# A two-layer graph transformer on one core: a longer weight ring from layer 1's output projection on, with tiles shared to make room, and PSUM banks and index work of layer 1's end in another order

## The chip, the core and the metric

The kernel runs on one core of a Trainium2 chip. The metric is device time in microseconds for one execution; below, "before" is the median of three executions. A core has five engines with instruction queues of their own: TensorE (PE in the profile, its weight loads PEld), VectorE (DVE), ScalarE (ACT), GpSimd (POOL) and SyncE (SP). Each queue is worked off in order; an instruction that waits holds up all behind it. DMA transfers are issued from the queues of SP, ACT and POOL and run beside the engines.

## The reference, cut to what matters

Everything is float32. There are 384 nodes with 1024 features and 12,288 edges. Each of two layers has a graph part, an attention-like part and a mixture of 8 experts. The change lies in the end of layer 0's experts and in layer 1:

```python
# layer 1 (x: 384 x 1024)
h     = normed(x) @ W                                   # graph attention, weights from edge counts
x    += elu(attention(h, a, src, dst))
q, k  = sigmoid(xn @ W_Q), sigmoid(xn @ W_K);  v = xn @ W_V
m     = linear_attention(q, k, v) @ W_fc + xn           # xn: the normed x from the layer's start
x    += gamma * normed(m) + beta
f     = normed(x);  e = argmax(f @ centroids.T)         # one expert of 8 for each node
g     = sigmoid(max(f @ centroids.T))
xe    = normed(f) * gamma[e] + beta[e]
out   = x + f + g * (relu(xe @ w1[e] + b1[e]) @ w2[e] + b2[e])
```

An expert's w1 is 1024 x 512 and its w2 is 512 x 1024: 2 MiB each, 16 such weights in layer 1's experts.

## The kernel before, in words

Nodes lie in three blocks of 128 (`nb`), features in 8 chunks of 128 (`kc`) or two halves of 512 (`hf`).

**Weights.** All large weights pass through a ring of SBUF places of 16 KB a partition (2 MiB in all). `next_w` (L103) takes the place at the front of the ring and moves it to the back; `load_w` (L117) and `load_t` (L107) issue one transfer into it from SyncE. A transfer may start when the last matmul that read the place's former weight is done. Three places are there from the start; `w_top` adds one, `w_more` two, so layer 1 runs with six. When the loads of the output projection `w_fc` have been written (L1145), the pool `mid` is closed (L1146), which frees the tiles that layer 1's middle needed, and a seventh place, `w_last`, is opened in their space (L1148, `LAST = 1`) and put at the front of the ring. The experts open an eighth, `w_end` (L1333), at the back; it lies where layer 1's tiles were and must wait until they are free.

Which instruction stands where in an engine's queue is decided by the Tile framework's scheduler when the program is built, from its estimate of when each can run; so SyncE's loads are not in the order of the source. `tc.issue_after(i)` asks it to put what follows behind instruction `i`. Tiles with the same tag in a pool share buffers, and a tile in a pool that opens over a closed one waits for the users of the closed pool.

**The end of layer 0's experts** (`experts0_sorted`, L889). Expert outputs go to DRAM (`yg0`), ordered by expert; each node gathers its two rows back with indirect DMAs from POOL (`take`, L984: two gathers and two VectorE multiply-adds, L989). For the second half of the features, the last two experts' outputs stay on chip and are added by matmuls with one-hot matrices `back` (L1032); the other experts' rows are gathered at the start of layer 1, block by block (L1039), and then normed (L1043, L1044), transposed and copied to `xnT` (L217), and multiplied by `W` (L1049).

**Layer 1's end.** For each block: two halves of the output projection (`project`, L1151), then `to_router` (L1182: norm, transposes to `xT`, scores against the centroids, moments, the twice-normed row `xn1` and the once-normed row `ft`), then `to_places` (L1205: best expert, place in the sorted order, scatter of the row to DRAM table `xg`; POOL then adds `ft` to `x`, L1224; for the last block VectorE does it, L1252). `to_first` (L1226) sorts the first 128 rows on chip by matmuls into two PSUM banks `first`; `scaled` (L997) multiplies by gamma and adds beta, the first half on VectorE (L1003, L1004), the second on ScalarE (L1010), into `xe0`. The values and node numbers of all sorted rows are scattered to DRAM table `ig`.

**Layer 1's experts** (`experts1_sorted`, L1331) run in four pairs. A pair's 128 rows (64 places for each of two experts) are loaded from `xg` by POOL (L1346), transposed (L1355) and scaled; pair 0's come from `xe0`. `hidden_of` (L1359) computes h with 16 matmuls (L1364; the profile shows two records for each), `hs` is its copy (half on VectorE, L1367, half on ScalarE, L1368), `by_feature` transposes it (L1376) and applies bias and relu, `give` (L1387) multiplies by w2 (y, L1395) and scatter-adds each half to `out` (L1398, L292). Around pair 0: `inf` is loaded from `ig`, three gathers fetch each node's b2 (L307), VectorE computes the target rows `half` (L1410) and adds b2 to `x` (L1412), and ScalarE stores x to `out` (L1414), block by block, ahead of the scatter-adds.

The PSUM pools of the experts are opened in the order transposes (4 banks), h (2), y (2), over layer 1's `pm` (4 banks, projections) and `px` (4 banks; `first` is among them).

Of the kernel before, what the change touches and what calls it, by code (L numbers as in the profile page):

```python
# [10 lines left out]
F32 = mybir.dt.float32  # L11
# [26 lines left out]
LAST = 1  # L38
# [7 lines left out]
def gps_two_layers(ctx: ExitStack, tc: tile.TileContext, d, out: bass.AP):  # L46
# [140 lines left out]
    def norm_on_act(dst, src, mean, rinv):  # L187

        off = small.tile([P, 1], F32, tag="off", name="off")
        ve.tensor_scalar(off, mean, rinv, -1.0, op0=OP.mult, op1=OP.mult)  # L190
        ac.activation(dst, src, AF.Identity, bias=off, scale=rinv)
# [62 lines left out]
    def gate_to_t(pool, tag, gate):  # L254
        gT = small.tile([X, N], F32, tag="gT", name="gT", bufs=1)
        ps = pool.tile([P, HB], F32, tag=tag, name="mm")
        for nb in range(NB):
            nc.tensor.transpose(ps[:X, nb * P:(nb + 1) * P], gate[:, nb, :], ident)
        ve.tensor_copy(gT, ps[:X, :N])
        return gT  # L260
# [153 lines left out]
    with ExitStack() as layer:  # L414
# [317 lines left out]
        def row(cols, name, dtype=F32):  # L732
# [4 lines left out]
                "slots": row([NB, 2], "slots6", I32), "share": row([2, NB], "share6"), "back": row([BACK, N], "back6"),  # L737
# [105 lines left out]
    def experts0_all():  # L843
        with tc.tile_pool(name="act1", bufs=1) as act, \
# [20 lines left out]
            gT = gate_to_t(pb, "b", oh[0])  # L865
# [23 lines left out]
    def experts0_sorted(keep):  # L889

        slots, share = keep["slots"], keep["share"]
        with tc.tile_pool(name="act6", bufs=1) as act, \
                tc.tile_pool(name="work6", bufs=2) as work, \
                tc.tile_pool(name="ps_t6", bufs=3, space=PSUM) as pt, \
                tc.tile_pool(name="ps_h6", bufs=5, space=PSUM) as ph:
# [35 lines left out]
            def ways_back():  # L931
# [19 lines left out]
                for e in range(BACK):  # L951
                    ac.copy(keep["back"][:, e, :], ps[e][:, :N])

            xeT = rows_of(0)
# [8 lines left out]
            for hf in range(2):  # L963
# [15 lines left out]
                if hf == 0:  # L979
                    for nb in range(NB):  # L980
                        yt = work.tile([P, 2, HB], F32, tag="yt", name="yt6", bufs=3)
                        take(hf, nb, yt, slots, share, X * CAP0)

# [13 lines left out]
    def scaled(dst, src, g, es):  # L997

        if g == 0:
            gm, bt = [gbx[:, i, es[0]:es[0] + 2, :4].rearrange("p r k -> p k r")[:, :, :, None].to_broadcast([P, 4, 2, CAP])  # L1000
                      for i in range(2)]
            to, of = [t.rearrange("p k (r c) -> p k r c", r=2) for t in (dst, src)]
            ve.tensor_tensor(to, of, gm, OP.mult)  # L1003
            ve.tensor_tensor(to, to, bt, OP.add)  # L1004
            return
        for j in range(4):
            for r, e in enumerate(es):
                cs = slice(r * CAP, (r + 1) * CAP)
                gm, bt = gbx[:, 0, e, 4 + j:5 + j], gbx[:, 1, e, 4 + j:5 + j]
                ac.activation(dst[:, j, cs], src[:, j, cs], AF.Identity, bias=bt, scale=gm)  # L1010

    def layer1(keep=None):


        with tc.tile_pool(name="act2", bufs=1) as act, \
# [5 lines left out]
            a_bc = act.tile([P, 2, D], F32, tag="rows", name="a_bc")  # L1021
            ed_w = part.tile([P, NB, N], F32, name="ed_w")
# [3 lines left out]
            hn = act.tile([P, NB, KC * K2V], F32, tag="rows3", name="hn")  # L1026
            ws = [load_w(d["w_gnn"][hf]) for hf in range(2)]
            taken, backs = None, []
            for nb in range(NB if keep is not None else 0):
                backs.append(px.tile([P, HB], F32, tag="x", name="back"))  # L1030
                for e in range(BACK):
                    mm(backs[nb], lhsT=keep["back"][:, e, nb * P:(nb + 1) * P],  # L1032
                       rhs=keep["xe0"][e].rearrange("p a b -> p (a b)"), start=e == 0, stop=e == BACK - 1)
            for nb in range(NB):
                with ExitStack() as behind:
                    if nb:
                        behind.enter_context(tc.issue_after(normed_half.ins))
                    if keep is not None:
                        taken = take(1, nb, work.tile([P, 2, HB], F32, tag="xn", name="yt1"),  # L1039
                                     keep["slots_g"], keep["share_g"], (X - BACK) * CAP0)  # L1040
# [30 lines left out]
            gb = act.tile([P, 2, D], F32, tag="rows", name="gb")  # L1071
            for i, n in enumerate(("gamma", "beta")):
                ac.dma_start(gb[:, i, :], bass.AP(tensor=d[n].tensor, offset=d[n].offset, ap=[[0, P], [1, D]]))

            kn = act.tile([P, NB, D], F32, tag="kq", name="kn")
# [14 lines left out]
            for b in range(NB):  # L1090
# [13 lines left out]
                gp.tensor_tensor(x[:, b, :], x[:, b, :], gb[:, 1, :], OP.add)  # L1104


            vn = act.tile([P, NB, KC * K2V], F32, tag="rows3", name="vn")
# [6 lines left out]
            kv = part.tile([P, KC, K2V], F32, name="kv")  # L1114
# [11 lines left out]
            qT = act.tile([P, KC, N], F32, tag="kq", name="qT2")  # L1126
# [32 lines left out]
            def mix_norm(nb):  # L1159
# [3 lines left out]
                for hf in range(2):  # L1163
                    cs = slice(hf * HB, (hf + 1) * HB)
                    ve.scalar_tensor_tensor(y[:, cs], xb[:, cs], mean, gb[:, 0, cs], op0=OP.subtract, op1=OP.mult)  # L1165
# [9 lines left out]
            ft = act.tile([P, NB, KC * K2V], F32, tag="rows3", name="ft4")  # L1175
            xT = act.tile([P, KC, N], F32, tag="kq", name="xT4")
# [5 lines left out]
            def to_router(nb):  # L1182
                mix_norm(nb)
                xs, xb, fb = x[:, nb, :], xn1[:, nb, :], ft[:, nb, :D]
                to_t(pm, xT, xs, nb)
                ps = px.tile([P, HB], F32, tag="x", name="x")
                for kc in range(KC):
                    mm(ps[:, :X], lhsT=xT[:, kc, nb * P:(nb + 1) * P], rhs=cen[:, kc, :],
# [13 lines left out]
                norm_on_act(fb, xs, mean, rinv)  # L1202
                sums[nb] = (ps, less, rinv)

            def to_places(nb):  # L1205
                xb, fb = xn1[:, nb, :], ft[:, nb, :D]
# [15 lines left out]
                if nb < NB - 1:  # L1222
                    with tc.issue_after(last[0].ins):
                        gp.tensor_tensor(x[:, nb, :], x[:, nb, :], fb, OP.add)  # L1224
# [27 lines left out]
            ve.tensor_tensor(x[:, NB - 1, :], x[:, NB - 1, :], ft[:, NB - 1, :D], OP.add)  # L1252
# [5 lines left out]
    def experts1_all():  # L1258
        with tc.tile_pool(name="act3", bufs=1) as act, \
# [41 lines left out]
            gT = gate_to_t(pb, "b", gate)  # L1301
# [29 lines left out]
    def experts1_sorted(xe0):  # L1331

        with tc.tile_pool(name="w_end", bufs=1) as w_end, \  # L1333
                tc.tile_pool(name="act4", bufs=1) as act, \
                tc.tile_pool(name="work5", bufs=2) as work, \
                tc.tile_pool(name="ps_t4", bufs=4, space=PSUM) as pt, \
                tc.tile_pool(name="ps_h4", bufs=2, space=PSUM) as ph, \
                tc.tile_pool(name="ps_y4", bufs=2, space=PSUM) as py:
            ring.append(w_end)
            inf = act.tile([P, X // 2, 2], F32, name="inf4")  # L1340
            half = act.tile([P, 2, X // 2], I32, name="half4")
            b2 = act.tile([P, NB, D], F32, name="b24")

            def load_rows(pair):
                xs = work.tile([P, D], F32, tag="xs", name="xs4", bufs=3)
                gp.dma_start(xs, xg[pair * P:(pair + 1) * P, :])  # L1346
                return xs

            def rows_of(pair):
                xeT = [work.tile([P, KC // 2, P], F32, tag=f"xeT{g}", name="xeT4") for g in range(2)]  # L1350
                for g in range(2):
# [4 lines left out]
                    scaled(xeT[g], ps, g, (2 * pair, 2 * pair + 1))  # L1356
                return xeT

            def hidden_of(pair, xeT):  # L1359
# [6 lines left out]
                hs = work.tile([P, F1], F32, tag="hs", name="hs4")  # L1366
# [4 lines left out]
            def by_feature(pair, hs):  # L1371
                hT = work.tile([P, F1 // P, P], F32, tag="hT", name="hT4")
# [14 lines left out]
            def give(pair, hT, between=None):  # L1387

                w2 = [load_w(d["xw2s"][e], (F1 // P, D)) for e in (2 * pair, 2 * pair + 1)]
                for hf in range(2):  # L1390
# [9 lines left out]
                    if hf == 0 and between is not None:  # L1400
                        got = rows_of(between)
                return got if between is not None else None

            xss = [None] + [load_rows(pair) for pair in range(1, X // 2)]
            gp.dma_start(inf, ig.rearrange("(a p) b -> p a b", p=P))
            for nb in range(NB):
                gather(b2[:, nb, :], d["b2"], keep["own_e"][:, nb:nb + 1], X)
            hs = hidden_of(0, xe0)
            for hf in range(2):
                ve.tensor_scalar(half[:, hf, :], inf[:, :, 1].bitcast(I32), 2.0, float(hf), op0=OP.mult, op1=OP.add)  # L1410
            for nb in range(NB):
                ve.scalar_tensor_tensor(x[:, nb, :], b2[:, nb, :], keep["info"][:, nb, 0:1], x[:, nb, :],  # L1412
                                        op0=OP.mult, op1=OP.add)
                ac.dma_start(out[nb * P:(nb + 1) * P, :], x[:, nb, :])  # L1414
            xeT = give(0, by_feature(0, hs), 1)
# [116 lines left out]
```

## Time and profile before

| | us |
|---|---|
| runs: median, lowest, highest | 1063.69, 1062.56, 1065.06 |
| the profiled execution: its time | 1065.01 |
| its span, first to last instruction | 1063.2 |
| TensorE busy in the span | 1023.2 |
| layer 1, from the first `back` matmul to pair 0's h | 700.9 to 979.1 |
| layer 1's experts, from pair 0's h to the last y | 979.1 to 1054.3 |
| from the last y to the span's end | 8.9 |

How to read what follows: a line of the timeline has the start and the length of a group of instructions in us from the span's start, the engine, the line in the source, the operation, what is written `<-` what is read, the shape and the number of instructions. In brackets stands how long the engine was idle before, and what ended that. A line of the waits has the waiting engine and line, what it waited for, the sum in us, how often and the longest. A line of the windows has the stretch, its length, the busy time of PE, PEld, DVE, ACT and POOL with the number of instructions, then the granted TensorE clock (1.00 is full), the busy share of the 16 DMA engines and the GB/s that they moved.

### The profile page before, as it was taken

The page shows a single profiled execution, that of the slowest core. Times are in us where ns is not written, and L with a number is a line of the kernel's source. Part 1 is how long each engine was busy: PE and PEld are TensorE (multiplying, and loading weights), DVE is VectorE, ACT ScalarE, POOL GpSimd, SP SyncE. Part 2 cuts the span into 40 slices and gives each one's busy share as a digit, 9 for nine tenths or more (in the row PEclk, how much of TensorE's full clock was granted, in tenths as well). Part 3 has the DMA queues.
Part 4 walks back from the last instruction along what each step waited for, and adds up shares of the span by engine and source line. Part 5 has one row for each costly group of instructions (what it writes and reads, how often), then busy time and mean ns, then how long its engine had stood idle before and what let it go on. Part 6 is the DMA issues. An engine that isn't in the chain of part 4 may idle for free. (4 is left out here: it accounts for less than half of the span.)

```text
span 1063.2 us, 9534 instructions
## 1 busy us (share of the span) xinstructions
PE 1023.2 (96%) x3455; PEld 557.6 (52%) x3455; DVE 356.4 (34%) x991; ACT 271.0 (25%) x501; POOL 325.2 (31%) x277
## 2 busy tenths in 40 slices
PE   6999999999999999999998999989999999998895
PEld 5555555554555555544466666434444465555352
DVE  4580000006666666711343111061306000474321
ACT  3111111110876666611121011221302010123120
POOL 2142466556686768510001000140002000013121
PEclk9999999999999999999997999989999999998999
DMA  9939523334425232533265898978522222425994
GB/s 345 393 141 365 154 80 100 139 105 99 80 1 118 42 80 1 159 86 123 92 210 201 305 311 293 380 265 291 198 80 79 80 80 79 158 74 198 398 383 118
DMA packets 69526, 182.84 MB, mean 172 GB/s; under 512 B 21488, under 2 KB 22352, under 8 KB 69216
## 3 DMA queue, kind: packets, MB, share of 16 engines
q1 hardware_dynamic: 40640, 146.01, 38.4%
q0 software_dynamic: 25120, 28.88, 11.6%
q10 hardware_dynamic: 3712, 7.27, 1.8%
q8 instruction: 29, 0.48, 0.2%
q14 instruction: 25, 0.20, 0.1%
HBM read 160.22 MB, written 22.44 MB: 172 GB/s over the span
## 5 line engine op out<-in xcount | busy, mean ns | idle before, releaser
L480 POOL DMA_INDIRECT countd<-seen,cells x96 | 154.3, 1608 | 64.3 <-DMA countd<-seen,cells 38.5
L135 PE MATMUL mm<-xnT,w 128*128 128x384 f32 x512 | 165.7, 486 | 0.1
L135 PEld LDWEIGHTS mm<-xnT,w 128*128 128x128 f32 x512 | 97.1, 190 | 67.6 <-DVE xnT L217 0.3
L666 PE MATMUL mm<-xnT,w 128*128 128x384 f32 x384 | 132.4, 493 | 0.0
L480 POOL DMA_INDIRECT lastd<-typ,cells x96 | 96.6, 1006 | 107.6 <-DMA lastd<-typ,cells 68.7
L666 PEld LDWEIGHTS mm<-xnT,w 128*128 128x128 f32 x384 | 70.5, 190 | 56.4 <-issue 13.4
L714 PE MATMUL mm<-w,t 128*128 128x512 f32 x192 | 84.3, 595 | 0.8 <-DVE x L402 0.8
L147 PE MATMUL mm<-w,xnT 128*128 128x512 f32 x192 | 82.8, 592 | 0.0
L135 PE MATMUL mm<-t,w 128*128 128x384 f32 x256 | 82.7, 486 | 0.0
L917 PE MATMUL h<-w,xeT 128*128 128x352 f32 x224 | 68.5, 462 | 0.6 <-DVE xeT L909 0.3
L135 PEld LDWEIGHTS mm<-t,w 128*128 128x128 f32 x256 | 48.6, 190 | 33.9
L147 PEld LDWEIGHTS mm<-w,xnT 128*128 128x128 f32 x192 | 36.3, 190 | 45.5 <-issue 45.5
L714 PEld LDWEIGHTS mm<-w,t 128*128 128x128 f32 x192 | 35.9, 190 | 44.1 <-issue 42.2
L586 DVE TENSOR_TENSOR kind<-last 128x1152 f32<-128x1152 f32 x1 | 1.4, 1358 | 165.7 <-DMA last<-lastd 165.7
L917 PEld LDWEIGHTS h<-w,xeT 128*128 128x128 f32 x224 | 41.8, 190 | 23.7 <-DVE xeT L909 2.1
L292 POOL DMA_INDIRECT xg<-xn,slot x3 | 4.0, 1342 | 140.4 <-DVE xn L1165 135.4
L1049 PE MATMUL mm<-w,xnT 128*128 128x512 f32 x96 | 44.9, 629 | 1.5 <-DVE xnT L217 1.5
L1154 PE MATMUL mm<-w,oT 128*128 128x512 f32 x96 | 42.6, 595 | 0.0
L969 PE MATMUL y<-w,hT 128*128 128x512 f32 (+1 forms) x96 | 41.6, 593 | 0.0
L147 PE MATMUL mm<-w,t 128*128 128x512 f32 x96 | 41.4, 592 | 0.0
L527 ACT ACTIVATE t<-mm,cols 128x384 f32<-128x384 f32 x24 | 14.0, 582 | 107.1 <-PE mm L135 102.5
L1104 POOL TENSOR_TENSOR x<-x,gb 128x1024 f32<-128x1024 f32 x3 | 7.3, 2427 | 100.8 <-DVE x L1103 100.8
(315 smaller groups left out, 1221.7 us busy)
## 6 DMA issues: line engine op xcount, KB each, us to landing
w<-in_w1s SPq DMA_DIRECT2D x16, 1408.0 KB
w<-in_xw SPq DMA_DIRECT2D x8, 2048.0 KB
w<-in_xw2s SPq DMA_DIRECT2D x8, 2048.0 KB
w<-in_w2s SPq DMA_DIRECT2D x8, 1536.0 KB
keys<-keyd POOLq DMA_DIRECT2D x4, 1536.0 KB
xg<-blank SPq DMA_DIRECT2D x12, 512.0 KB
xs<-xg POOLq DMA_DIRECT2D x10, 512.0 KB
w<-in_wk SPq DMA_DIRECT2D x2, 2048.0 KB
```

The source lines that it names most:

```text
L135: mm(ps[:, :N], lhsT=w[:, j, kc, :], rhs=rhs[:, kc, :], start=kc == 0, stop=kc == KC - 1)
L147: mm(ps, lhsT=lhs[:, kc, nb * P:(nb + 1) * P], rhs=w[:, kc, :], start=i == 0 and kc == 0, stop=i == len(pairs) - 1 and kc == KC - 1)
L292: i = gp.indirect_dma_start(rows, bass.IndirectOffsetOnAxis(ap=at, axis=0), src, None, bounds_check=n - 1, oob_is_err=False, compute_op=op)
L480: gp.indirect_dma_start(cells[:, :], bass.IndirectOffsetOnAxis(ap=at[:, i, c:c + 1], axis=0), src[:, c:c + 1], None, bounds_check=N * N + ...
L527: ac.activation(dst[:, ob, :], ps, AF.Identity, bias=cols[:, i, ob:ob + 1], scale=1.0)
L666: mm(ps[:, :N], lhsT=w[:, j, kc, :], rhs=xnT[:, kc, :], start=kc == 0, stop=kc == KC - 1)
L714: mm(pss[hf], lhsT=src[:, kc, nb * P:(nb + 1) * P], rhs=w_out[("mwo", "wo")[part]][hf][:, kc, :], start=part == 0 and kc == 0, stop=part = ...
L917: mm(ag[i][:, :F0], lhsT=xeT[kc // 4][:, kc % 4, :], rhs=w1[kc // 4][:, kc % 4, i * F0:(i + 1) * F0], start=kc == 0, stop=kc == KC - 1)
L969: mm(y, lhsT=hT[:k, e, j, :], rhs=w2[:k, e % 2 * len(K2) + j, :], start=j == 0, stop=j == len(K2) - 1)
L1049: mm(ps, lhsT=xnT[:, kc, nb * P:(nb + 1) * P], rhs=ws[hf][:, kc, :], start=kc == 0, stop=kc == KC - 1)
L1104: gp.tensor_tensor(x[:, b, :], x[:, b, :], gb[:, 1, :], OP.add)
L1154: mm(ps, lhsT=oT[:, kc, nb * P:(nb + 1) * P], rhs=ws[hf][:, kc, :], start=kc == 0, stop=kc == KC - 1)
```

## The change

- `LAST` becomes 3, and `w_end` goes. From layer 1's output projection on the ring has nine places, all but three of them as before; the three `w_last` stand at the front.
- To make room, tiles move into `mid` and share: `a_bc` with `kn` and `qT`; `hn` and `vn`; `ed_w` with `kv`. `gamma` and `beta` are two tiles, loaded by POOL behind the last gather instead of by ScalarE. `back` shares the tile `own` and one more. `xT` is a work tile of one block. `ft` goes: `add_normed` computes x + f in place on ScalarE, as x * (rinv + 1) - mean * rinv, so the adds on POOL (L1224) and VectorE (L1252) go.
- In layer 0's experts and in layer 1's, the PSUM pools are opened in another order: h's and y's banks first, the transposes' last.
- Block 0's gather of the second half (`take_back`) moves from layer 1 to the end of layer 0's experts.
- In layer 1's experts, pair 1's rows are transposed right after pair 0's `by_feature` and before pair 0's w2 matmuls; `half`, the b2 adds and the stores of x come behind the scaling of pair 1's first half, and the stores move to SyncE. The rows of pairs and the b2 gathers share four buffers, so the rows of pairs 2 and 3 are loaded after pair 1's are used. `hs` and `hT` have one buffer instead of two.

```diff
-LAST = 1
+LAST = 3
...
-    def norm_on_act(dst, src, mean, rinv):
+    def add_normed(x, mean, rinv):
         off = small.tile([P, 1], F32, tag="off", name="off")
         ve.tensor_scalar(off, mean, rinv, -1.0, op0=OP.mult, op1=OP.mult)
-        ac.activation(dst, src, AF.Identity, bias=off, scale=rinv)
+        more = small.tile([P, 1], F32, tag="more", name="more")
+        ve.tensor_scalar(more, rinv, 1.0, None, op0=OP.add)
+        ac.activation(x, x, AF.Identity, bias=off, scale=more)
...
-                tc.tile_pool(name="ps_t6", bufs=3, space=PSUM) as pt, \
-                tc.tile_pool(name="ps_h6", bufs=5, space=PSUM) as ph:
+                tc.tile_pool(name="ps_h6", bufs=5, space=PSUM) as ph, \
+                tc.tile_pool(name="ps_t6", bufs=3, space=PSUM) as pt:
...
+            take_back(work.tile([P, D], F32, tag="xs", name="yt1").rearrange("p (a b) -> p a b", b=HB), 0)
+
+    def take_back(yt, nb):
+        return take(1, nb, yt, keep["slots_g"], keep["share_g"], (X - BACK) * CAP0)
...
-            a_bc = act.tile([P, 2, D], F32, tag="rows", name="a_bc")
-            ed_w = part.tile([P, NB, N], F32, name="ed_w")
+            ed_w = part.tile([P, NB, N], F32, tag="ed", name="ed_w")
...
-            hn = act.tile([P, NB, KC * K2V], F32, tag="rows3", name="hn")
+            hn = part.tile([P, NB, KC * K2V], F32, tag="rows3", name="hn")
+            a_bc = part.tile([P, NB, D], F32, tag="kq", name="a_bc")[:, :2, :]
...
-                        taken = take(1, nb, work.tile([P, 2, HB], F32, tag="xn", name="yt1"),
-                                     keep["slots_g"], keep["share_g"], (X - BACK) * CAP0)
+                        if nb:
+                            taken = take_back(work.tile([P, 2, HB], F32, tag="xn", name="yt1"), nb)
...
+            gamma, beta = act.tile([P, D], F32, name="gamma"), part.tile([P, D], F32, name="beta")
+            with tc.issue_after(taken.ins) if taken else ExitStack():
+                for to, n in ((gamma, "gamma"), (beta, "beta")):
+                    gp.dma_start(to, bass.AP(tensor=d[n].tensor, offset=d[n].offset, ap=[[0, P], [1, D]]))
...
-                norm_on_act(fb, xs, mean, rinv)
+                add_normed(xs, mean, rinv)
...
-                if nb < NB - 1:
-                    with tc.issue_after(last[0].ins):
-                        gp.tensor_tensor(x[:, nb, :], x[:, nb, :], fb, OP.add)
...
-            ve.tensor_tensor(x[:, NB - 1, :], x[:, NB - 1, :], ft[:, NB - 1, :D], OP.add)
...
-        with tc.tile_pool(name="w_end", bufs=1) as w_end, \
-                tc.tile_pool(name="act4", bufs=1) as act, \
+        with tc.tile_pool(name="act4", bufs=1) as act, \
                 tc.tile_pool(name="work5", bufs=2) as work, \
-                tc.tile_pool(name="ps_t4", bufs=4, space=PSUM) as pt, \
                 tc.tile_pool(name="ps_h4", bufs=2, space=PSUM) as ph, \
-                tc.tile_pool(name="ps_y4", bufs=2, space=PSUM) as py:
-            ring.append(w_end)
+                tc.tile_pool(name="ps_y4", bufs=2, space=PSUM) as py, \
+                tc.tile_pool(name="ps_t4", bufs=4, space=PSUM) as pt:
...
-            xss = [None] + [load_rows(pair) for pair in range(1, X // 2)]
+            xss = {1: load_rows(1)}
             gp.dma_start(inf, ig.rearrange("(a p) b -> p a b", p=P))
             for nb in range(NB):
-                gather(b2[:, nb, :], d["b2"], keep["own_e"][:, nb:nb + 1], X)
+                b2s.append(work.tile([P, D], F32, tag="row", name="b24", bufs=4))
+                gather(b2s[nb], d["b2"], keep["own_e"][:, nb:nb + 1], X)
+            xss.update({pair: load_rows(pair) for pair in (2, 3)})
             hs = hidden_of(0, xe0)
-            for hf in range(2):
-                ve.tensor_scalar(half[:, hf, :], inf[:, :, 1].bitcast(I32), 2.0, float(hf), op0=OP.mult, op1=OP.add)
-            for nb in range(NB):
-                ve.scalar_tensor_tensor(x[:, nb, :], b2[:, nb, :], keep["info"][:, nb, 0:1], x[:, nb, :],
-                                        op0=OP.mult, op1=OP.add)
-                ac.dma_start(out[nb * P:(nb + 1) * P, :], x[:, nb, :])
-            xeT = give(0, by_feature(0, hs), 1)
+            hT = by_feature(0, hs)
+            xeT = rows_of(1)
+            with tc.issue_after(scaled_by[0].ins):
+                for hf in range(2):
+                    ve.tensor_scalar(half[:, hf, :], inf[:, :, 1].bitcast(I32), 2.0, float(hf), op0=OP.mult, op1=OP.add)
+                for nb in range(NB):
+                    ve.scalar_tensor_tensor(x[:, nb, :], b2s[nb], keep["info"][:, nb, 0:1], x[:, nb, :],
+                                            op0=OP.mult, op1=OP.add)
+                    nc.sync.dma_start(out[nb * P:(nb + 1) * P, :], x[:, nb, :])
+            give(0, hT)
```

## The prediction

> **What bounds the kernel now.** I read the page first, then TensorE's waits, then the timelines of the stretches where it waits, last the windows with the DMA share.
>
> ```profile
> span 1063.2 us, 9534 instructions
> PE 1023.2 (96%) x3455; PEld 557.6 (52%) x3455; DVE 356.4 (34%) x991; ACT 271.0 (25%) x501; POOL 325.2 (31%) x277
> ```
>
> TensorE is busy for 96% and the change takes no matmul away. All that it can win is among the 40.0 us of idle time and in stretches at half clock. TensorE's waits after 800 us:
>
> ```profile
> PE t L1376 <- issue: 3.9, 1, 3.9
> PE h L1364 <- ACT xe L1010: 2.6, 1, 2.6
> PE first L1228 <- DVE slot L1219: 1.7, 2, 1.2
> PE y L1395 <- SPq L1430: 1.7, 1, 1.7
> ```
>
> Three of these lie in the last experts, which the change rebuilds. TensorE's timeline there (start, length, [idle before]):
>
> ```profile
> 979.08 8.78 PE L1364 MATMUL h<-w,xe 128*64 128x512 f32 x32 [2.57 <-ACT xe L1010]
> 991.72 0.84 PE L1376 MATMUL t<-ident,hs 128*128 128x128 f32 x4 [3.86 <-issue]
> ...
> 1002.26 7.03 PE L1364 MATMUL h<-w,xeT 128*64 128x512 f32 x32
> ...
> 1042.81 0.84 PE L1376 MATMUL t<-ident,hs 128*128 128x128 f32 x4 [0.94 <-DVE hs L1367]
> 1043.69 1.93 PE L1395 MATMUL y<-w,hT 128*64 128x512 f32 x4
> 1047.28 7.05 PE L1395 MATMUL y<-w,hT 128*64 128x512 f32 x28 [1.65 <-SPq L1430]
> ```
>
> Pair 0's h takes 8.78 us where pair 1's takes 7.03. "issue" before 991.72 is explained by VectorE's timeline: the copy of hs stands in its queue behind half, which needs inf from DRAM.
>
> ```profile
> 975.65 1.22 DVE L1252 TENSOR_TENSOR x<-x,ft 128x1024 f32<-128x1024 f32 x1
> 976.79 0.68 DVE L1004 TENSOR_TENSOR xe<-xe,gbx 128x512 f32<-128x512 f32 x1
> 991.05 0.24 DVE L1410 TENSOR_SCALAR half<-inf 128x4 int32<-128x4 int32 x2 [13.58 <-DMA b<-in_b,own_e]
> 991.20 0.42 DVE L1367 COPY hs<-h 128x256 f32<-128x256 f32 x1
> ```
>
> The last wait (1.65 us) is for pair 3's second w2. The windows (last two columns: DMA share, GB/s) show why it is late:
>
> ```profile
> 905.00:950.00 45.00, 44.21 (x175) 25.32 (x175) 25.70 (x88) 7.35 (x12) 1.92 (x2) 1.00 0.27 94
> 950.00:978.00 28.00, 24.44 (x132) 18.70 (x130) 17.81 (x69) 9.58 (x18) 9.30 (x6) 0.88 0.55 207
> 978.00:988.00 10.00, 8.78 (x32) 2.61 (x32) 0.00 (x0) 1.03 (x4) 4.50 (x7) 0.83 0.97 313
> 988.00:1046.50 58.50, 52.87 (x236) 24.53 (x236) 17.12 (x37) 12.64 (x44) 11.57 (x8) 0.97 1.00 372
> ```
>
> From 978 to 1046.5 the DMA engines have no free time; from 905 to 978 they have much. So the tail has two limits close together: TensorE's chain, and the bytes that may only be asked for when a place comes free.
>
> **The change, part by part.** *Places.* Before, SyncE issues w2 of pair 1 at 977.26 (the place w_end opens only when layer 1's pools close) and pair 2's first w1 at 987.89. So 9 tiles of 2.1 MB cross the full stretch. In the built order of the changed program, SyncE issues pair 0's w1, w1 and w2 into the three shared places at about 912 (the release of before's w_last: 912.34), and the places that they would have taken go to later tiles. Pair 1's last w2 goes at 951.6, pair 2's first w1 at 961.4, when out-projection weights are done. From the end of pair 0's h on, 7 tiles are left instead of 9. The two go where the share was 0.27 to 0.55.
>
> *Pair 0's h.* Its PSUM bank comes from a pool that no longer overlaps first, and L1252 is gone from VectorE. Pair 0's first half is ready at 975.05 + 0.69 + 0.68 = 976.4, plus 0.12 for the new small operation more (three of them, like L1196's 0.15 us rows; two are hidden under projection matmuls); TensorE ends first at 976.5 + 0.1. The second half on ScalarE ends at 979.0 as before, when 16 of the 32 matmul records have 3.5 us of work. So h starts at 976.6: 2.5 us won. The in-place activation of x costs what L191 does now (1.23 us, same shape). Two adds on POOL (2.38 us each) go and were hidden.
>
> *Clock.* The page "TensorE: Matmul & The Clock Gate" of the Trainium skill (HAM oscillation) asks for no idle gap over about 3.4 us; a gap of 2.57 us would then cost its own length alone. The trace says otherwise: 713 ns a record in pair 0's h against 592 in the others, clock 0.83 in that window, so 8.78 against 7.03. I take the row, 1.75 us won; by the rule it is 0, and the total below shrinks by 1.7. The end of h moves from 987.86 to 983.6.
>
> *half.* It is placed behind pair 1's scaling, so hs is copied at once: the wait 3.86 becomes pair 3's 0.94; 2.9 us won. Then hs transposes 0.84, xs transposes 1.76 (now ahead of y), y 7.3 as in pair 1, against 10.54 us from 991.72 to 1002.26: about 0.7 us won, again clock. Pair 1's h starts at 994.4 instead of 1002.26. Pair 1's rows are issued at 979 as now, and land near 983 on idle DMA engines; they are needed at 985.3.
>
> *TensorE's chain after that* is unchanged: 41.4 us from pair 1's h to pair 3's y. So y could start at 1035.8 instead of 1043.69.
>
> *Supply.* Bytes from 978 to 1046.5: 10 x 313 + 58.5 x 372 = 24.9 MB, of which 9 tiles are 18.9 and rows, gathers, stores and scatters 6.0. From 983.6 on, 7 tiles (14.7) and about 5.4 of the others are left: 20.1 MB at 372 GB/s is 54.0 us, to 1037.6. Now 0.7 us lie between the last packets and 1047.28; so TensorE resumes at 1038.3 instead of 1047.28: 9.0 us won, with a stall of some 2.5 us left. The page "DMA: Bandwidth & Descriptors" (Specifications) gives about 358 GB/s of HBM to a core; that would mean 56.1 us, and 2.1 less won. The row is measured in this very stretch, so I take 372.
>
> *SyncE's queue.* Out's three stores (0.35 us each) move from ScalarE's queue to SyncE's, ahead of pair 2's w2, and wait for the three gathers of b2. Behind them stand six tile loads. Now the gathers' last user starts at 999.13, but with 4.2 MB queued at 988 beside them; with 2.1 MB I expect 991 to 993. Until then pair 2's second w1 and the gathers keep DMA busy. Bounds: no loss, and 6 us if the gathers land as late as now. I take 0.
>
> *The other places.* Block 0's gather (take_back) moves ahead of layer 1. Before and after it:
>
> ```profile
> 700.07 1.00 POOL L307 DMA_INDIRECT yt<-yg,slots_g  x1 [4.78 <-DVE x L989]
> ...
> 706.05 1.00 POOL L307 DMA_INDIRECT yt<-yg,slots_g  x1 [0.67 <-DVE x L989]
> ```
>
> It no longer waits for VectorE's last L989 (ends 699.17), but still for the landing of the last yg rows (packets until 698.4): 0.4 us won. Block 1's gather, now at 702.68, is then the one that waits for the old pool, whose last reader ends at 705.78: it goes at about 705.7, and 700.07 to 703.77 says 3.7 us until its use, so 709.4. On VectorE its use and one BN_STATS stand ahead of the copy of block 0's xnT, which TensorE awaits: 709.99 becomes about 710.7 to 711.0. Net +0.6 us; below, -3 us if the shorter idle keeps the clock (now half for 6.8 us from 709.9), above, +2 if the gather is slower. gamma and beta move to POOL's queue behind the same gathers (some 0.6 us each, as a_bc's row); POOL is then idle for 94 us before its next add, and the edge counts behind them are needed only at 764. a_bc now shares with kn: its last reader ends at 762, kn is first written at 765.8. The reordered banks of layer 0's experts give nothing: their first h still waits for ScalarE.
>
> Sum: -9.0 + 0.6 = -8.4. The profiled execution took 1065.01 us about a span of 1063.2, at the upper end of its three runs; from the median 1063.69 I get 1055.3 us.
>
> **Rivals.**
> 1. *TensorE alone bounds the tail* (stores or scatters give way, or the clock holds at 710): y starts at 1035.8, which is -11.4 + 0.6 to -11.4: 1052.4. For it: only the last tile is short, by 2.5 us. Against it: the share of 1.00.
> 2. *Stores block SyncE.* If the gathers land as now, the six loads go at about 1000.7, DMA stands still for 3 to 6 us, and the end is 1058.5 to 1061. For it: an in-order queue. Against it: half the competing bytes.
> 3. *The change doesn't do what it says*: the deeper ring only moves the wait, total within 0.2%. The chain of 8 us in front of pair 1 speaks against it, since these gains need no place.
> 4. *Slower: the shared places are not free at 912.* SyncE is in order; pair 0's w1 stands ahead of everything later. If one of the three places waited for layer 1's end, as w_end does at 977.26, twelve tiles at 5.6 us and 6 MB of others would follow: 31 MB at 372 is 84 us, to 1061, and the end at 1077. It decides at about 965: two tiles must land by 976.6. Against it: all tiles that these places overlay have their last reader before 912.
>
> **How the numbers follow.** Forecast 1055.3, own range 1053.5 to 1057.5, chance 0.50. Rival 1: 0.18. Rival 2: 0.16, most of it still faster by over 0.2%. Rival 3: 0.06. Rival 4 or anything like it: 0.10. The measurement can tell about 0.2% (2.1 us) from no change. Faster 0.81, within 0.2% 0.09, slower 0.10. Range: down to rival 1 with a kept clock, up to most of rival 2: 1051.5 to 1060.5.
>
> **What would show it.** Right: no ScalarE wait before pair 0's h and a length near 7.0; under 1.2 us before its hs transposes; pair 1's h near 995; three w loads close together near 912; a DMA share near 1 from 984 to 1038 and a last wait for a w2 of 1 to 3 us. A wait of about 2 us before L1058's first matmul shows the gather's price. Wrong: idle DMA near 995 (stores), no last wait (TensorE bounds), or loads bunched after 970.

## The result, and the profile after

Ten runs each: 1058.34 us median (1057.05 to 1060.3) against 1062.33 us before (1060.72 to 1065.06). The ratio is 0.9962, with a 95% interval of 0.9951 to 0.9972: 4.0 us faster. A second set gave 1059.55 us (12 runs) against 1062.21 (17 runs), ratio 0.9971 (0.9962 to 0.9981). The forecast of 1055.3 had the sign and the mechanism; its gain was too large: 1058.34 lies 0.8 us outside the own range of 1053.5 to 1057.5 and inside the wide one. The 1063.69 us that stood for before in the forecast is the median of the first three of these ten runs. The profiled execution after took 1058.17 us, with this page head:

```profile
span 1056.4 us, 9529 instructions
PE 1019.2 (96%) x3455; PEld 554.2 (52%) x3455; DVE 356.2 (34%) x993; ACT 270.6 (26%) x501; POOL 320.3 (30%) x277
```

Line numbers are now those of the changed kernel (y is L1402, h L1371, the projection of layer 1's start L1058). TensorE's waits from 940 us on:

```profile
PE y L1402 <- SPq L1439: 2.4, 1, 2.4
PE first L1234 <- DVE slot L1228: 1.9, 2, 1.4
PE h L1371 <- SPq L1439: 1.4, 1, 1.4
PE t L1383 <- DVE hs L1374: 1.1, 2, 0.6
```

The waits of 2.6 us for ScalarE and of 3.9 us in front of pair 0's hs transposes are gone. Two waits for weights are left, both in pair 3. TensorE's timeline in the experts:

```profile
975.88 8.30 PE L1371 MATMUL h<-w,xe 128*64 128x512 f32 x32
984.74 0.84 PE L1383 MATMUL t<-ident,hs 128*128 128x128 f32 x4 [0.56 <-DVE hs L1374]
...
993.30 7.04 PE L1371 MATMUL h<-w,xeT 128*64 128x512 f32 x32
...
1027.57 7.08 PE L1371 MATMUL h<-w,xeT 128*64 128x512 f32 x30 [1.40 <-SPq L1439]
...
1036.11 1.93 PE L1402 MATMUL y<-w,hT 128*64 128x512 f32 x4
1040.44 7.05 PE L1402 MATMUL y<-w,hT 128*64 128x512 f32 x28 [2.41 <-SPq L1439]
```

Pair 0's h starts with no wait, but still takes 8.30 us. The last y resumes at 1040.44; 1038.3 was forecast. The granted clock (third column from the end) around the start of h, first in before, where h starts at 979.08, then in after, where it starts at 975.88:

```profile
970.00:976.00 6.00, 4.82 (x23) 4.72 (x23) 3.35 (x23) 3.68 (x5) 1.97 (x2) 0.50 0.15 61
976.50:979.00 2.50, 0.01 (x1) 0.00 (x0) 0.97 (x2) 2.45 (x8) 2.19 (x3) 1.00 0.43 51
980.00:982.50 2.50, 2.50 (x8) 0.73 (x6) 0.00 (x0) 0.00 (x0) 0.65 (x2) 0.50 0.96 335
```

```profile
972.00:978.00 6.00, 5.84 (x22) 4.26 (x24) 1.62 (x5) 3.41 (x9) 4.17 (x5) 0.50 0.23 88
```

Before has two spells at half clock: one in the router, which ends before h starts, and one that begins 0.5 us into h. After has the router's alone, but h now starts inside it. The windows of after (last two columns: DMA share, GB/s):

```profile
905.00:950.00 45.00, 44.20 (x175) 25.18 (x174) 25.89 (x89) 7.28 (x12) 1.55 (x1) 1.00 0.50 188
950.00:978.00 28.00, 25.42 (x138) 18.63 (x138) 16.24 (x70) 10.33 (x20) 5.65 (x6) 0.88 0.55 206
978.00:984.00 6.00, 6.00 (x28) 1.68 (x24) 0.00 (x0) 0.46 (x2) 3.97 (x5) 0.97 0.67 142
984.00:1040.00 56.00, 51.43 (x238) 22.42 (x236) 17.14 (x37) 12.23 (x44) 10.87 (x9) 1.00 0.98 354
```

Two tiles moved into the stretch from 905 to 950, whose rate doubled from 94 to 188 GB/s. From 984 on the engines are full again, until the last transfers run out from 1036 on; the mean is 354 GB/s.

### The profile page after: what moved, and what is told of

It is laid out like the page before. It is cut to its first block, busy times and chain, and to the rows that moved or that the text cites. A ratio compares the mean times of both kernels' runs of the same rounds, so it can differ in the third digit from the quotient of the medians.

```text
span 1056.4 us, 9529 instructions
## 1 busy us (share of the span) xinstructions
PE 1019.2 (96%) x3455; PEld 554.2 (52%) x3455; DVE 356.2 (34%) x993; ACT 270.6 (26%) x501; POOL 320.3 (30%) x277
## 5 line engine op out<-in xcount | busy, mean ns | idle before, releaser
L1058 PE MATMUL mm<-w,xnT 128*128 128x512 f32 x96 | 43.9, 617 | 1.9 <-DVE xnT L219 1.9
L1114 POOL TENSOR_TENSOR x<-x,beta 128x1024 f32<-128x1024 f32 x3 | 7.3, 2428 | 97.5 <-DVE x L1113 97.5
## 6 DMA issues: line engine op xcount, KB each, us to landing
xg<-blank SPq DMA_DIRECT2D x12, 512.0 KB, 11.3
```

The lines of the kernel that those rows point to most:

```text
L1058: mm(ps, lhsT=xnT[:, kc, nb * P:(nb + 1) * P], rhs=ws[hf][:, kc, :], start=kc == 0, stop=kc == KC - 1)
L1114: gp.tensor_tensor(x[:, b, :], x[:, b, :], beta, OP.add)
```

## The experiments

**How they are compared.** Runs of one program differ by 2 to 11 us, and the time at which the router ends (`first`) wanders between 972.6 and 976.7 us from trace to trace. So the table counts from the end of `first` (972.16 + 3.79 = 975.95 in the trace of after) to the moment when the last y resumes behind its weight (1040.44), which leaves everything ahead of the experts out. The rest of y is 28 of its 32 matmul records (30 in f1 and f3, all 32 in e2 and g2). Two numbers in a cell are two traces or two sets of runs. The medians come from four sets, whose own medians of before were 1062.33 us (after), 1063.08 (e1 to e4), 1061.62 (f1 to f3, e3b) and 1062.21 (g0 to g2, after again); each ratio is to the runs of before in the same set.

| kernel | weight places | last y resumes, us after `first` | length of the rest of y, us | median us | ratio to before, 95% |
|---|---|---|---|---|---|
| before | 8, the last opens at 977 | 70.8; 71.4 | 7.05; 7.05 | 1062.33 | 1 |
| after | 9 | 64.5; 64.0 | 7.05; 7.05 | 1058.34; 1059.55 | 0.9962; 0.9971 |
| e1: gather back in layer 1 | 9 | 64.7 | 8.58 | 1057.21 | 0.9935 (0.9914 to 0.9957) |
| e2: half, b2, stores early | 9 | no wait | 7.27 | 1058.93 | 0.9970 (0.9956 to 0.9983) |
| e3: 7 places | 7 | 75.5 | 7.05 | 1069.35 | 1.0053 (1.0033 to 1.0074) |
| e3b: 8 places | 8 | 69.8 | 8.75 | 1062.91 | 1.0005 (0.9995 to 1.0015) |
| e4: old PSUM order | 9 | 66.7 | 8.75 | 1060.23 | 0.9968 (0.9955 to 0.9980) |
| f1: stores on ScalarE | 9 | 64.5 | 10.03 | 1058.20 | 0.9963 (0.9950 to 0.9976) |
| f2: b2 gathers ahead of inf | 9 | 62.5 | 7.05 | 1054.75 | 0.9933 (0.9919 to 0.9947) |
| f3: e1, f1 and f2 | 9 | 63.6 | 8.43 | 1056.43 | 0.9953 (0.9936 to 0.9970) |
| g1: e1 and f2 | 9 | 61.8 | 8.75 | 1054.49 | 0.9923 (0.9907 to 0.9939) |
| g2: one tile left out | 9 | no wait | 7.27 | 1054.33 | 0.9924 (0.9909 to 0.9940) |

My theory was that the bytes set the end: from pair 0's h on, the DMA engines are full, and only fewer bytes from there on, or an earlier start, move it. The rivals were that TensorE's own chain sets it, and that the stores block SyncE.

### The places: e3 and e3b

```diff
-LAST = 3
+LAST = 1
```

and `LAST = 2` in e3b.

> After, with 7 instead of 9 weight places in the end of layer 1 (the named constant back at 1). Theory A (the supply of weights sets the end, as the waits of 1.40 and 2.41 us on SyncE's queue say): two tiles fewer are in place when the end begins, each 2.1 MB or 5.9 us at the 354 GB/s measured, 11.8 us in all, of which some 7 us beyond what the page before showed is not possible: the end returns to before's 1047.3 for the last resumption or later, so +5 to +8 us, about 1064 to 1066 us. Rival B (the places decide little, and the order of PSUM banks and of the index step carry the gain): +0 to +2 us.

> After, with 8 weight places in the end of layer 1 instead of 9 (7 gave 1069.35 us against 1058.34). Theory A (bytes: each place is one tile of 2.1 MB less in the full stretch, at about 390 GB/s 5.4 us): 1063.8 us, the middle between the two, and as slow as before. Rival B (the loss with 7 places came from the loads' order behind the stores): most of it comes with the last place taken away, so less than 3 us above after, 1059 to 1061 us.

TensorE's timeline of e3:

```profile
1017.56 9.84 PE L1371 MATMUL h<-w,xeT 128*64 128x512 f32 x30 [7.75 <-DMA w<-in_xw]
1051.33 7.05 PE L1402 MATMUL y<-w,hT 128*64 128x512 f32 x28 [2.20 <-SPq L1439]
```

and of e3b:

```profile
1020.95 8.23 PE L1402 MATMUL y<-w,hT 128*64 128x512 f32 x29 [3.47 <-DMA w<-in_xw2s]
1044.03 8.75 PE L1402 MATMUL y<-w,hT 128*64 128x512 f32 x28 [2.42 <-SPq L1439]
```

By the table, 7, 8 and 9 places end their supply at 75.5, 69.8 and 64.3 us: 5.7 and 5.5 us a place, which is 2.1 MB at about 375 GB/s. In time it is 11.0 us by the medians and 9.7 by the ratios for two places (I expected 5 to 8), and 4.6 by both for one (5.4). My cap for e3 was wrong: 7 places are fewer than before had, since before's eighth, though it opens only at 977, gives SyncE a load for the stretch up to 984, in which the DMA engines otherwise have room (from 978 to 984 their share is 0.94 in before and 0.46 in e3). And e3b, with every other edit of the change in it, is as slow as before. Of the change's parts, the ninth place is what the time shows.

### The waits that went: e4 and e2

```diff
+                tc.tile_pool(name="ps_t4", bufs=4, space=PSUM) as pt, \
                 tc.tile_pool(name="ps_h4", bufs=2, space=PSUM) as ph, \
                 tc.tile_pool(name="ps_y4", bufs=2, space=PSUM) as py, \
-                tc.tile_pool(name="ps_t4", bufs=4, space=PSUM) as pt:
```

> After, with the order of PSUM pools in layer 1's end as before the change, so that pair 0's hidden product takes over banks that the router used last. Theory A (bank handover was the 2.5 us wait of before in front of pair 0's hidden product, and the supply hides part): the wait is there again in the trace (1.5 to 2.5 us), and the time rises by 0 to 1 us because TensorE is early there and late only on weights afterwards. Rival B (TensorE's own work sets the end): +1.5 to +2.5 us, about 1060.5 us. Rival C (the wait belongs to VectorE's slot step and not to the banks): no wait comes back, 0.

TensorE's timeline of e4, then two of its windows:

```profile
979.24 8.78 PE L1371 MATMUL h<-w,xe 128*64 128x512 f32 x32 [2.57 <-ACT xe L1019]
1043.33 8.75 PE L1402 MATMUL y<-w,hT 128*64 128x512 f32 x28 [2.72 <-SPq L1439]
```

```profile
978.00:984.00 6.00, 4.76 (x15) 1.47 (x17) 0.00 (x0) 1.19 (x5) 4.22 (x5) 0.72 0.48 93
984.00:988.00 4.00, 4.00 (x20) 1.15 (x16) 0.00 (x0) 0.00 (x0) 1.10 (x2) 1.00 0.92 282
```

The wait of 2.57 us is back to the hundredth, so the order of the banks was its cause. As in before, half clock follows it inside h (a granted clock of 0.50 from 980 to 982.5). The supply ends 2.2 us later (66.7 against 64.5), although the same tiles are in place: the next load waits for the place that pair 0's h gives back, at 988.0 here and 984.2 in after, and until then the DMA engines have room. So a wait in front of *this* matmul does cost supply. In time the ratios, 0.9968 against 0.9962, do not tell it from nothing, and the medians put it at 0.7 to 1.9 us: not settled.

e2 writes the following block ahead of pair 0's transposes, and not behind pair 1's scaling:

```diff
             hs = hidden_of(0, xe0)
+            for hf in range(2):
+                ve.tensor_scalar(half[:, hf, :], inf[:, :, 1].bitcast(I32), 2.0, float(hf), op0=OP.mult, op1=OP.add)
+            for nb in range(NB):
+                ve.scalar_tensor_tensor(x[:, nb, :], b2s[nb], keep["info"][:, nb, 0:1], x[:, nb, :],
+                                        op0=OP.mult, op1=OP.add)
+                nc.sync.dma_start(out[nb * P:(nb + 1) * P, :], x[:, nb, :])
             hT = by_feature(0, hs)
```

> After, with the index step (half), the b2 additions and the three output stores written ahead of pair 0's transposes again, as before the change. Theory A (the step's place was worth what TensorE waited there before): TensorE waits 2.5 to 3.5 us for VectorE in front of pair 1's hidden product or pair 0's second transposes again, and because the weights from pair 1 on are late by 3.8 us in all whatever TensorE does, only the part above that shows in the time: 0 to +1 us. Rival B (TensorE's own work sets the end): the whole wait shows, +2.5 to +3.5 us, about 1061.5 us. Rival C (the place was worth nothing, the wait of before was the index data's arrival): no wait, 0.

```profile
988.25 1.05 PE L1383 MATMUL t<-ident,hs 128*128 128x128 f32 x4 [3.79 <-DVE hs L1374]
...
1040.01 0.84 PE L1383 MATMUL t<-ident,hs 128*128 128x128 f32 x4 [0.59 <-DVE hs L1374]
1040.89 7.27 PE L1402 MATMUL y<-w,hT 128*64 128x512 f32 x32
```

The wait is back (3.79 us), both weight waits are gone, and the last y is done at 1048.16, where after's is done at 1047.49. The time moved by less than 1 us (0.6 by the medians, 0.8 by the ratios). This is theory A at its plainest: what TensorE loses early it no longer waits for late.

### SyncE's queue: f1

```diff
-                    nc.sync.dma_start(out[nb * P:(nb + 1) * P, :], x[:, nb, :])
+                    ac.dma_start(out[nb * P:(nb + 1) * P, :], x[:, nb, :])
```

> After, with the three stores of out back on ScalarE's queue (as before the change) instead of SyncE's. Theory A (bytes: from about 981 us on the DMA engines are full, so a tile load that SyncE issues 4 to 12 us earlier only shares the same rate): the two or three tile loads behind the stores are issued at 985 to 993 instead of 992 to 997, and the time stays within 1 us of after, 1058.3. Rival B (the stores block SyncE and so the supply): the last wait for a w2 loses what the blocked loads were late, 2 to 4 us faster, about 1055.3. Rival C (the loads that are freed push the gathers of b2 aside, and the stores and scatters behind them come later): up to 2 us slower.

SyncE's queue in after:

```profile
988.83 3.16 SPq L1423 DMA_DIRECT2D out<-x  x3
992.08 1.80 SPq L124 DMA_DIRECT2D w<-in_xw2s  x2
```

and in f1:

```profile
982.69 0.37 SPq L124 DMA_DIRECT2D w<-in_xw  x1
983.15 9.20 SPq L124 DMA_DIRECT2D w<-in_xw2s  x2
```

The stores do block: a place was free at 984.2, and the w2 load went at 992.1. Counted from the end of `first`, it goes 7.5 us earlier without them (8.6 against 16.1). But it lands only 0.6 us earlier (31.0 against 31.6), and the last y resumes at the same 64.5. Time: 1058.20, unchanged. A load that was issued early into full DMA engines bought nothing.

### Small transfers ahead of big ones: f2 and g1

```diff
-            gp.dma_start(inf, ig.rearrange("(a p) b -> p a b", p=P))
             for nb in range(NB):
                 b2s.append(work.tile([P, D], F32, tag="row", name="b24", bufs=4))
                 gather(b2s[nb], d["b2"], keep["own_e"][:, nb:nb + 1], X)
+            gp.dma_start(inf, ig.rearrange("(a p) b -> p a b", p=P))
```

> After, with the small load of inf issued behind the three gathers of b2 on GpSimd's queue, not ahead of them. Theory A (bytes): the gathers start about 978.4 instead of 980.6, in a stretch where the DMA engines are at a share of 0.13, so 1 to 2 us of their work leaves the full stretch, and the last weights come 1 to 2 us earlier: 1056.3 to 1057.3 us. Rival B (the b2 gathers are not what the DMA engines are full of): within 0.5 us of 1058.3. Rival C (inf is then late and VectorE waits for it at half): half starts after 990, with the stores behind it 2 to 4 us later, and the time 0 to 2 us above after.

The windows of after, and then that of f2, in which the gathers of b2 run:

```profile
984.00:988.00 4.00, 3.44 (x22) 1.90 (x22) 3.11 (x10) 2.70 (x11) 0.92 (x2) 1.00 0.95 260
988.00:992.00 4.00, 4.00 (x20) 1.29 (x18) 3.65 (x4) 0.98 (x4) 0.55 (x1) 1.00 1.02 402
```

```profile
984.00:988.00 4.00, 3.92 (x24) 2.12 (x26) 2.17 (x7) 3.36 (x13) 0.55 (x1) 1.00 1.01 382
```

In after the load of inf waits 1.1 us on GpSimd's queue for the scatters to `ig`, and the gathers stand behind it. They then share the DMA engines with the first tile load: share 0.95 at 260 GB/s, against 402 four microseconds later. With the gathers ahead of inf that window carries 382 GB/s, the supply ends at 62.5 instead of 64.0 to 64.5, and the time falls by 3.6 us in the medians and by 0.0029 in the ratio (3.1 us), more than the 1 to 2 us that I expected. The three traces with this edit end their supply at 61.8 to 63.6, the four with nine places and neither this edit nor e4's at 64.0 to 64.7. (Pair 0's h ended 0.9 us earlier in this trace, at full clock; in e1 it did too, and the supply still ended at 64.7.) VectorE then does wait for inf (2.20 us, until 989.0), but TensorE waits no longer for it. The trace explains 1.5 to 2.0 us of the gain; the rest is not in it (the traced execution, 1056.20 us, was one of the two slow ones of its five).

g1 adds to f2 the next experiment's edit:

> After, with inf behind the gathers of b2 and block 0's gather back inside layer 1; the stores stay on SyncE. Theory A (the two gains of 1.1 and 3.6 us come from different places and add): 1053.7 us. Theory B (an earlier TensorE meets the same last weights later, as with all three edits together, 1056.43): no gain over 1054.75, 1054.5 to 1056.5.

```profile
1035.93 8.75 PE L1400 MATMUL y<-w,hT 128*64 128x512 f32 x28 [2.19 <-SPq L1437]
```

It is the fastest version that computes the whole result: 1054.49 us, ratio 0.9923, 5.1 us under after on the same chip. But it is no better than f2 by more than the intervals. That is nearer to theory B (1054.5 to 1056.5) than to A (1053.7), but an interval of 1.7 us either way doesn't tell them apart. In the trace everything ahead of the last y is earlier, and behind the last wait the clock is half. f3, which puts the stores on ScalarE as well, went the same way:

> After, with three edits together: block 0's gather back inside layer 1, the stores on ScalarE's queue, and inf behind the gathers of b2. Theory A (bytes): the gather's place is worth about 1 us (57.2 instead of 58.3 in the earlier run), inf 1 to 2 us, the stores nothing: about 1055.8 us. Rival B (stores block SyncE): 1053 us or less.

It measured 1056.43 us; its last wait is 3.18 us, followed by 8.43.

### Block 0's gather: e1

```diff
-            take_back(work.tile([P, D], F32, tag="xs", name="yt1").rearrange("p (a b) -> p a b", b=HB), 0)
...
-                        if nb:
-                            taken = take_back(work.tile([P, 2, HB], F32, tag="xn", name="yt1"), nb)
+                        taken = take_back(work.tile([P, 2, HB], F32, tag="xn", name="yt1"), nb)
```

> After, with block 0's gather and weighting of layer 1's start put back inside layer 1 (as before the change); everything else as after. Theory A (the gathers' new order costs VectorE's xnT copy its place, as the trace of after shows with waits of 3.04 and 1.15 us at the start of layer 1): this start gets 0.5 to 1 us shorter, so 0.5 to 1 us below after, about 1057.6 us. Rival B (the early gather saves the 0.4 us that SP and GpSimd need, and the copy was not late): 0.4 us above after. Rival C (the place of the gather means nothing): within 0.2 us of after.

The start of layer 1 in after, TensorE and then VectorE:

```profile
708.53 1.84 PE L218 MATMUL mm<-ident,xn 128*128 128x128 f32 x8 [3.04 <-DVE xn L204]
711.52 15.98 PE L1058 MATMUL mm<-w,xnT 128*128 128x512 f32 x32 [1.15 <-DVE xnT L219]
```

```profile
709.52 0.75 DVE L999 SCALAR_TENSOR_TENSOR x<-yt,share_g,x 128x512 f32<-128x512 f32 x1 [1.04 <-DMA yt<-yg,slots_g]
710.19 0.69 DVE L170 BATCH_NORM_STATS2 bst<-x 128x6 f32<-128x512 f32 x1
710.79 0.67 DVE L219 COPY xnT<-mm 128x512 f32<-128x512 f32 x1
```

and TensorE's in e1:

```profile
709.02 1.97 PE L218 MATMUL mm<-ident,xn 128*128 128x128 f32 x8 [3.77 <-DVE xn L204]
710.92 16.15 PE L1056 MATMUL mm<-w,xnT 128*128 128x512 f32 x32
```

The copy that TensorE awaits stands on VectorE behind block 1's multiply-add, which waits 1.04 us for its gather. From the first `back` matmul to the projection it is 11.4 and 11.7 us in the two traces of after and 11.3 to 12.4 in the seven others with the gather moved; it is 11.1, 10.1 and 10.7 in e1, f3 and g1, which have it back in place, and 9.9 and 10.9 before. So the move costs this stretch about 1 us, as theory A says. In the time e1 gains 1.1 us by the medians and 2.9 by the ratios, with an interval that overlaps that of after's first set; how much it is stays open.

### The last tile: g2, and before once more: g0

```diff
-                w2 = [load_w(d["xw2s"][e], (F1 // P, D)) for e in (2 * pair, 2 * pair + 1)]
+                w2 = [load_w(d["xw2s"][e], (F1 // P, D)) for e in (2 * pair, 2 * pair + 1)[:1 if pair == X // 2 - 1 else 2]] * (2 if pair == X // 2 - 1 else 1)
```

> After, with pair 3's second w2 left out (both halves of the last product use the first one, so out differs for one expert). Theory A (bytes set the end): the last wait, 2.41 us, goes, and the time is 1055.5 to 1056 us. Rival B (TensorE alone bounds the tail): the same as after. How much more than 2.4 us it wins says what the wait cost in clock.

> The kernel before once more, for a second trace of it. Theory A (the wait of 2.57 us in front of pair 0's hidden product is followed by a stretch at half clock, as in the first trace): the product takes 8.2 to 8.8 us again, and the wait for the last w2 ends near 1047 less whatever the span is shorter. Theory B (where the stretches at half clock fall is an accident of the run): 7.1 us, and a span near 1060.5.

> The kernel after once more, beside the others on one chip, and for a second trace. Expected: 1057.5 to 1059 us; a wait for the last w2 of 2 to 4 us, and where it is over 3 us, a last product that takes longer than 7.1 us.

TensorE's timeline of g2:

```profile
1027.08 7.08 PE L1371 MATMUL h<-w,xeT 128*64 128x512 f32 x30 [2.35 <-SPq L1439]
...
1035.62 7.27 PE L1402 MATMUL y<-w,hT 128*64 128x512 f32 x32
```

and of g0:

```profile
975.19 9.67 PE L1364 MATMUL h<-w,xe 128*64 128x512 f32 x32 [2.58 <-ACT xe L1010]
...
1044.05 7.05 PE L1395 MATMUL y<-w,hT 128*64 128x512 f32 x28 [1.87 <-SPq L1430]
```

Without its last tile the kernel takes 1054.33 us, 4.0 and 5.2 us under the two medians of after, though its wait was only 2.4. g0 (one execution) took 1061.44 us at a span of 1059.7. Its h took 9.67 us behind the wait, longer than expected; here the clock had been at 0.50 since 967, in the router, and stayed there until 980. From the end of `first` its last y resumes after 71.4 us (70.8 in the first trace), so before's tail is the same in both; the 3.5 us between the two spans lie almost wholly ahead of it, where `first` ended at 976.5 in the first trace and at 972.6 here. The second trace of after is like its first, with a last wait of 2.29 us and a last y of 7.05, at a span of 1055.3. It took 1057.13 us, the least of its 12 runs; their median of 1059.55 is 0.55 us above what I expected.

## Why the prediction was right, and where its size was off

**Bank order, half, and TensorE's chain: right.** h at the end of `first` with no wait; 0.56 us in front of the hs transposes (0.94 expected); pair 1's h 17.4 us behind pair 0's (17.8); y could start at 1036.1 (1035.8). That last agreement is in part luck, since 1036.1 holds a wait of 1.40 us for pair 3's w1 that was not forecast. Little of this shows in the time: e3b has all of it and is as fast as before, and e2 lacks one part and loses less than 1 us. For the banks, e4 leaves it open between 0 and 1.9 us.

**The supply term was mis-sized.** The step "20.1 MB at 372 GB/s is 54.0 us, to 1037.6" had the bytes right (354 GB/s over 56 us are 19.8 MB) and the rate wrong. From the end of h at 984.2 to the last packets at 1039.8 it took 55.6 us, 1.6 us more; the other 0.6 us of the delay to 1040.44 is that h ended later than 983.6. The row of 372 began at 988; in after, the full stretch begins with the gathers of b2, at 260 GB/s. Against 372 these 4 us lose 1.2 us; the rest lies behind 988, where 362 GB/s were moved. I set aside the 358 GB/s of the Trainium skill's page "DMA: Bandwidth & Descriptors" (Specifications) for the row; the estimate of 56.1 us from it was nearer than my 54.0. That does not make 358 a ceiling: single windows reached 402 to 421, and before moved 388 from 988 to 1040. The tail, from the end of `first` to the end of the last y, fell from 77.8 and 78.5 us to 71.5 and 71.1: 6.9 us on average, where 9.0 were forecast.

**The clock term: half right.** Of the 1.75 us for pair 0's h ("I take the row") little came: h took 8.30 and 8.24 us in after. The spell at half clock behind the wait is gone, as forecast. But I had read the length of h alone, and not the clock ahead of it: before's trace has 0.50 in the router too, until 976.2, and an h that starts right behind `first` meets the end of that spell. In after it lasts until 978.4. In the other kernels without the wait h took 7.09 us where the spell ended before it and up to 8.18 where it did not; in the three traces with the wait it took 8.78, 9.67 and 8.78. By the rule of the Trainium skill's page "TensorE: Matmul & The Clock Gate" (HAM oscillation), which asks only that no gap be over about 3.4 us, the gap of 2.57 us costs no clock; in before and in e4 the clock was back at 1.00 in the gap and fell to 0.50 within 0.6 us of the start of h, which it does in none of the eleven traces without the gap. In g0 it was half all along, so this trace does not show it.

**Block 0's gather: right in kind,** +0.6 us forecast, about +1 us measured; the copy that TensorE awaits came at 710.79, where 710.7 to 711.0 was forecast. **The stores:** the 0 was right, and so was its reason: they held SyncE for 7.5 us, until 992.1 (991 to 993 expected), and until then the first tile and the gathers kept the DMA engines at a share of 0.95 and more. f1 shows that the delay did not matter.

**The sum.** With 6.9 in the tail and 1 lost at the start, the gain is about 5.9 us, and the traces agree: spans of 1063.2 and 1059.7 became 1056.4 and 1055.3, 5.6 us less on average. The timed runs show 4.0 and 2.7 us. The forecast had also set a gain that was read from one trace against the median of three runs, 1063.69; that median is 1.4 us above the one of all ten. The 2 to 3 us in between come from which executions were traced: the two of before are 1.0 us above the medians of their sets on average, the two of after 1.3 us below. What varies there between executions stays open. A cause that fits, but is only argued: in half of the twelve traces with a last wait the last y, after it, ran at half clock (0.50) for a time and took 1.4 to 3.0 us longer. Neither trace of after had this; others of its runs may (spans of 1055.2 us at a mean clock of 0.987 to 1058.5 at 0.984). g2 points the same way, as it has no such wait and wins more than the wait's length.

**The rivals.** Rival 1 (TensorE alone) would have left g2 as slow as after; with the last tile away it is 4.0 to 5.2 us faster, so the last tile's arrival set the end. Rival 2's blocking came, but without its price; that 1058.34 lies next to its 1058.5 to 1061 is chance, since f1 has no blocking and the same time. Rival 4 did not happen: the shared places took their three loads at 912.2 to 913.3. Rival 3's picture, a wait that only moves, is true of e2's part alone.

## What to carry to other kernels

Where a stretch is full of transfers, count bytes from the moment at which the first place comes free: a place more was worth one tile's transfer time, 5.5 to 5.7 us of supply. A shorter wait on the compute engine was swallowed by the later wait for weights (e2), but not one in front of the matmul that gives the first place back (e4: 2.2 us of supply). Look then for small transfers at the edge of the full stretch and put them ahead of it; one line in GpSimd's queue was worth nearly as much as the whole change. When a gain of under 1% is read from one trace, align the traces at an event ahead of the change, and do not subtract from a median what the profiled run alone may have lost. Before a wait's removal is credited with clock, look at the clock ahead of the wait.

## What was not expected of the hardware

- The length of a gap alone does not tell whether half clock follows. The last y took 7.05 us, at a granted clock of 1.00 in after, following waits of 2.41, 2.29, 2.20, 1.87 and 1.65 us, and 8.43 to 10.03, with 0.50 from 1039 to 1044 in f1, following 2.19, 2.38, 2.42, 2.72, 3.18 and 3.90.
- A spell at half clock does not need a long gap. In after the clock fell to 0.50 near 971.5, in the router's small matmuls; TensorE had been idle for at most 0.5 us at a time in the 10 us ahead, and for some 0.8 us when it fell. All 14 traces have such a spell there.
- A busy share is no rate: 0.95 went with 260 GB/s where gathers run beside a tile load, and 1.02 to 1.03 with 402 to 421 GB/s where tiles run with stores of 0.5 MB.
